# Seventeen unread TensorE products around the first attention scores of layer 1, in a four-layer float32 network on one core

## The chip, the core and the metric

The kernel runs on one core of a Trainium2 chip. The metric is the device time of one execution in microseconds (us); lower is better. Three runs of the kernel before took 2797.55, 2802.72 and 2804.87 us, so the median is 2802.72 us. Besides, one execution was taken by the hardware profiler; all positions below ("at 519 us") are microseconds from the start of that execution's span.

## What is computed

Four layers work on `x` of shape (8, 512, 128), in float32. Each layer is half a feed-forward step, an attention step and half a feed-forward step again, each on a layer-normalised copy:

```python
x = x + 0.5 * L0_ffn(norm(x));  x = x + L0_attn(norm(x));  x = x + 0.5 * L0_ffn(norm(x))
x = x + 0.5 * L1_ffn(norm(x));  x = x + L1_attn(norm(x));  x = x + 0.5 * L1_ffn(norm(x))
...                                                          # layers 2 and 3 likewise
```

The stretch that matters here is the passage from the end of layer 0 to layer 1's attention. That attention has 16 heads of width 8 with rotary positions:

```python
q, k, v = heads(x @ Wq + bq), heads(x @ Wk + bk), heads(x @ Wv + bv)
q, k = rope(q), rope(k)
probs = softmax(q @ k.T / sqrt(8))
out = probs @ v  ->  merged heads @ Wo + bo
```

L1's feed-forward step routes each token to one of 64 small splines by two rounds of scores, a table lookup and an argmax, and normalises its result.

## The kernel before

The input is held on chip as eight blocks `x[b]`, each of 512 rows as 128 partitions x 4 x 128. A normalised copy of block b is `xn[b]`, and its transpose is `xt[b]` (128 partitions, 512 columns). TensorE's order of work is written out by hand in two ways: a dictionary `todo` maps a place (a number) to the steps that are issued there, and it is run in ascending order of places.

*The passage*, `l0_tail` (L810), fetches layer 0's second expert results, adds them, normalises the blocks by pairs (`pair`, L203) and runs the front of L1's feed-forward step for all blocks. For blocks 0 and 1 it also runs the whole step (`l1_ffn_steps`, L920): for block 1 its later places are 55.5 (`turn`, L986, two transposes on TensorE and a copy on ScalarE), 57.5 (`spline`, whose table is a product at L996), 60 (`direct`, a second table product and VectorE work), 62.5 (the statistics, `measure` at L161 on VectorE and GpSimd, then ScalarE, L842) and 69 (`update`, VectorE, L1030 and L1031). Block 0 enters the attention from the list `enter`: at 51.5 its normalised copy is transposed (L237), at 52.5 and 53.5 it is projected to q and k (`project`, L1086: two products each at L1092, rotation on VectorE at L1098 and L1101, then a write to DRAM and a read back into `q` or `k` through SyncE's DMA queue), and at 55 to v (`values`, L1109). The PSUM tiles of the passage come from one pool of seven banks, handed out in turn.

*The attention*, `l1_block` (L1038), goes through 128 units, four for each of the four head groups of each of the eight blocks. In a unit `first` (L1124) is called twice (h = 0 and 1). Each call makes one score tile of two heads, 128 queries by 512 keys each, in one of two PSUM buffers, and VectorE reduces it to the row maxima (L1131). The products of `first` contract over 32 partitions, of which nine are in use. A product in float32 shows as two MATMUL records in the trace, so a unit has eight records of L1130. Eleven units later (`LAG`) `second` (L1145) makes the transposed scores again, with the maxima already subtracted, and ScalarE takes their exponential. So the first eleven units consist of `first` alone, with a few steps of the feed-forward of block 2 and the entry of block 1 between them (`works`). The dictionary of these steps is also called `todo`, and its key is 2n + h for unit n. At key 1 it has `outset` (L1115), which makes a bias with one product (L1120) and one VectorE addition (L1121).

[...]

Of the kernel before, what the change touches and what calls it, by code (L numbers as in the profile page):

```python
# [108 lines left out]
class Net:  # L109
# [700 lines left out]
    def l0_tail(self, w1, wk, bank, room, clear, enter):  # L810

        todo = {}
        load, both, add = self.returned(wk, self.yds[1], 4)

        def at(n, work, *args):
            todo.setdefault(n, []).append(lambda: work(*args))

        for g in range(4):
            n = 9 * g
            for k in range(2):  # L820
                b = 2 * g + k
                at(n - 30, load, b)
                at(n + 1.3 * k, both, b)
                at(n + 1.5 + 1.3 * k, add, b)
                squeeze, finish = self.l1_ffn_front(b, w1, bank, lambda name, shape, k=k: wk.tile([P, *shape], F32, tag=f"{name}{k}", name=name))
                self.plan(todo, (n + 16 + 1.5 * k, n + 19 + 1.5 * k), lambda _, b=b, squeeze=squeeze: squeeze(self.xt[b]), finish)
            self.pair(todo, g, n + 3.5, bank)
        at(20, clear, 0)
        at(46, clear, 1)
        for b, n in ((0, 0), (1, 26)):  # L830
            twin = lambda name, shape: wk.tile([P, *shape], F32, tag=name, name=name)
            self.plan(todo, [n + k for k in (14.7, 17, 18, 19.5, 20.5, 21.7, 23.5, 24.5, 25.5, 27, 28, 29.5, 31.5, 34, 36.5, 43)],
                      *self.l1_ffn_steps(b, w1, bank, twin if b else room, self.xn[b], self.xt[b], self.soon))
        self.plan(todo, (44.5, 51.5, 52.5, 53.5, 55), lambda _: self.soon(0, self.xn[0]), lambda xn: self.turned(xn, bank, self.xt[0]), *enter)
        self.run(todo)

    def soon(self, b, out, src=None):

        src = self.x[b] if src is None else src
        nb, rs = self.measure([src], True)  # L840
        for i in range(4):
            self.nc.scalar.activation(out[:, i, :], src[:, i, :], AF.Identity, bias=nb[:, i : i + 1], scale=rs[:, i : i + 1])  # L842
        return out
# [194 lines left out]
    def l1_block(self, w, w2, room, pool_w):  # L1038
# [18 lines left out]
        with ExitStack() as c:  # L1057
# [10 lines left out]
                nc.sync.dma_start(out=s[8], in_=a["zero"].rearrange("(h n) -> h n", n=512))  # L1068
                scrs.append(s)
            nms, prs, ats = {}, {}, {}  # L1070
            later, todo, bo = {}, {1: [lambda: outset()]}, []

            def clear(n):
                nc.gpsimd.memset(qs[n], 0.0)
# [5 lines left out]
            def bank(name, shape=(P, 512)):  # L1080
                return ps.tile(list(shape), F32, tag="s2", name=name, bufs=4)
# [33 lines left out]
            def outset():  # L1115

                made = pool.tile([P, 2, P], F32, tag="bo", name="bo")
                nc.gpsimd.tensor_scalar(made[:, 0, :], self.const("ones"), self.col("l1_bv"), None, ALU.mult)
                bp = bank("bp", (P, P))
                nc.tensor.matmul(bp, lhsT=made[:, 0, :], rhs=wv[:, 1, :], start=True, stop=True)  # L1120
                nc.vector.tensor_tensor(made[:, 1, :], bp, self.row("l1_bo"), ALU.add)  # L1121
                bo.append(made[:, 1, :])
# [79 lines left out]
            for b in range(NB):  # L1202
                n = 32 * b
# [6 lines left out]
            for b in range(2):  # L1210
                n = 32 * (NB + b) - 50
# [3 lines left out]
            n = 32 * NB - 50 + 32  # L1215
# [664 lines left out]
```

## Time and profile before

| what | value |
|---|---|
| median of three runs | 2802.72 us |
| the profiled execution's own time | 2823.91 us |
| its span, first to last instruction | 2821.98 us |
| mean granted TensorE clock | 0.939 |
| busy: TensorE, VectorE, ScalarE, GpSimd | 89%, 67%, 62%, 42% |
| passage (`l0_tail`) | about 417 to 519 us |
| first scores alone (units 0 to 10) | 519 to 569 us |
| TensorE and VectorE busy from 519 to 569 us | 44.6 and 32.0 of 50 us |
| granted clock from 519 to 569 us | 0.50 |

How to read it: the profiled execution takes some 21 us more than the median run, so a sum of durations is made against 2823.91 us, and only its difference is carried over. "Granted clock" is the share of TensorE's full clock that it was allowed in a stretch; in this trace it takes the values 0.50 and 1.00, and a number between them is a mean over both. PE is TensorE, PEld its loading of weights, DVE VectorE, ACT ScalarE, POOL GpSimd and SPq the queue of SyncE, which issues DMAs. In a row of the timeline, `x8` is the number of records merged into it, and a bracket at its end gives how long the engine sat idle before and who ended that.

### The profile page before, as it was taken

How to read it: one execution, taken by the hardware profiler on the slowest of the kernel's cores; microseconds unless marked ns; L12 is line 12 of the kernel's file. 1: busy time of each engine (PE TensorE's matmuls, PEld its weight loads, DVE VectorE, ACT ScalarE, POOL GpSimd, SP SyncE). 2: the span in 40 equal slices, each digit the busy share in tenths (PEclk: the TensorE clock that was granted, in tenths of full speed). 3: DMA queues.
4: the chain of work that ended last, by engine and by line, in shares of the span. 5: the costliest groups of instructions: out<-in, count | busy, mean ns of one | idle time of the engine just before them, and what ended most of it. 6: DMA issues, size and time to landing. Idle time of an engine off the chain costs nothing.

```text
span 2822.0 us, 51514 instructions
## 1 busy us (share of the span) xinstructions
PE 2508.1 (89%) x18564; PEld 1500.6 (53%) x18564; DVE 1886.6 (67%) x5099; ACT 1741.5 (62%) x4302; POOL 1177.3 (42%) x2073
## 2 busy tenths in 40 slices
PE   5667685799999998899999999999989999999996
PEld 5445453333333343456566656566555666666663
DVE  5235424677777763465666666655589888998897
ACT  2124124166666665676666666666578888988884
POOL 5644356333333442225425344250244454554442
PEclk9877785599999998999999999999999999999998
DMA  8121132000000000000000000000000000000000
GB/s 255 42 68 32 41 89 74 17 17 18 21 19 19 10 18 4 31 1 1 1 1 1 1 1 1 1 1 1 16 9 9 17 20 17 9 17 20 20 2 12
DMA packets 74349, 67.28 MB, mean 24 GB/s; under 512 B 17760, under 2 KB 63848, under 8 KB 71880
## 3 DMA queue, kind: packets, MB, share of 16 engines
q1 hardware_dynamic: 66128, 51.44, 6.8%
q0 software_dynamic: 3872, 8.11, 1.1%
q10 hardware_dynamic: 4096, 4.44, 0.5%
q8 instruction: 148, 2.42, 0.4%
q14 instruction: 105, 0.86, 0.1%
HBM read 36.68 MB, written 27.33 MB: 23 GB/s over the span
## 4 chain that ended last, share of the span: by engine, by line
PE 52%; DVE 16%; ACT 10%; POOL 4%; issue 2%; DMA 0%; SPq 0%; POOLq 0%; ACTq 0%; DVEq 0%
PE tp L1313 7%; PE s L1287 5%; PE s L1130 5%; PE o L1602 4%; PE o L1160 4%; ACT e L1560 4%; PE o L1329 4%; DVE nm L1131 4%; PE s L1553 3%; DVE nm L1291 3%; PE yp L308 3%; PE tp L1579 2%; DVE x L310 2%; PE op L1616 2%; ACT pt L1581 2%
## 5 line engine op out<-in xcount | busy, mean ns | idle before, releaser
L1131 DVE TENSOR_REDUCE nm<-s 128x2 f32<-128x1024 f32 x256 | 305.7, 1218 | 126.7 <-PE s L1150 114.1
L1298 ACT ACTIVATE e<-s,nm 128x512 f32<-128x512 f32 x512 | 344.9, 688 | 26.8 <-DVE nm L1291 22.2
L1152 ACT ACTIVATE pr<-s 128x512 f32<-128x512 f32 x512 | 272.2, 599 | 116.6 <-PE s L1150 106.4
L1319 ACT ACTIVATE p<-tp 128x512 f32<-128x512 f32 x512 | 279.3, 616 | 69.2 <-PE tp L1313 69.2
L1130 PE MATMUL s<-k,q 32*128 32x512 f32 x1024 | 291.4, 676 | 33.6 <-DVE nm L1131 29.2
L1291 DVE TENSOR_REDUCE nm<-s 128x2 f32<-128x1024 f32 x256 | 301.0, 1217 | 27.7 <-PE s L1287 25.8
L1313 PE MATMUL tp<-cst,e 128*128 128x128 f32 x2048 | 293.6, 282 | 24.7 <-DVE rs L1304 14.3
L1313 PEld LDWEIGHTS tp<-cst,e 128*128 128x128 f32 x2048 | 220.4, 142 | 163.0 <-issue 97.8
L1150 PE MATMUL s<-q,k 32*128 32x512 f32 x1024 | 292.1, 639 | 10.4 <-ACT pr L1152 8.6
L1307 POOL TENSOR_SCALAR e<-e,rs 128x512 f32<-128x512 f32 x114 | 199.8, 1753 | 235.5 <-DVE rs L1304 196.0
L1560 ACT ACTIVATE e<-e,m 128x512 f32<-128x512 f32 (+3 forms) x512 | 286.1, 570 | 14.1 <-DVE m L1557 14.0
L1557 DVE CUSTOM_DVE_ANT_0 e<-s,bias 128x512 f32<-128x512 f32 (+3 forms) x512 | 220.1, 486 | 76.6 <-PE s L1553 76.3
L173 POOL TENSOR_TENSOR d<-st 128x4 f32<-128x4 f32 (+2 forms) x97 | 19.8, 204 | 557.1 <-DVE st L170 478.1
L1581 ACT COPY pt<-tp 128x512 f32<-128x512 f32 x320 | 173.8, 590 | 83.4 <-PE tp L1579 83.3
L1307 DVE TENSOR_SCALAR e<-e,rs 128x512 f32<-128x512 f32 x398 | 195.4, 521 | 9.1
L310 DVE SCALAR_TENSOR_TENSOR x<-yp,sel,x 128x128 f32<-128x128 f32 x512 | 178.0, 348 | 31.4 <-PE yp L308 18.8
L1287 PE MATMUL s<-k,q 32*128 32x512 f32 x1024 | 175.1, 648 | 4.8 <-issue 2.5
L1553 PE MATMUL s<-qk 64*128 64x512 f32 (+3 forms) x1024 | 172.7, 456 | 3.1 <-DVE m L1557 2.0
L1579 PE MATMUL tp<-cst,e 128*128 128x128 f32 x1280 | 169.1, 278 | 4.3 <-ACT k L1021 2.6
L1130 PEld LDWEIGHTS s<-k,q 32*128 32x128 f32 x1024 | 88.5, 195 | 153.0 <-DVE nm L1131 102.8
L1329 PE MATMUL o<-p,va 128*32 128x128 f32 x4096 | 165.4, 277 | 2.6 <-ACT p L1319 2.6
L1579 PEld LDWEIGHTS tp<-cst,e 128*128 128x128 f32 x1280 | 139.8, 142 | 39.0 <-issue 14.8
(408 smaller groups left out, 4981.9 us busy)
## 6 DMA issues: line engine op xcount, KB each, us to landing
yd<-z SPq DMA_DIRECT2D x8, 1024.0 KB
r<-yd SPq DMA_DIRECT2D x32, 256.0 KB
xd<-xn SPq DMA_DIRECT2D x16, 256.0 KB
k<-sk SPq DMA_DIRECT2D x64, 64.0 KB
sk<-pu SPq DMA_DIRECT2D x16, 256.0 KB
w<-in_l_w SPq DMA_DIRECT2D x14, 256.0 KB
q<-sq SPq DMA_DIRECT2D x32, 72.0 KB
x<-in_x SPq DMA_DIRECT2D x8, 256.0 KB
```

The source lines that it names most:

```text
L1130: nc.tensor.matmul(s[:, jj, :], lhsT=q[cut, g, i * P : (i + 1) * P], rhs=k[cut, g, :], start=True, stop=True)
L1131: nc.vector.tensor_reduce(nms[b, g // 2][:, i, 2 * h : 2 * h + 2, g % 2], s, AX.X, ALU.max, negate=True)
L1150: nc.tensor.matmul(s, lhsT=k[cut, g, kt * P : (kt + 1) * P], rhs=q[cut, g, :], start=True, stop=True)
L1287: nc.tensor.matmul(s[:, jj, :], lhsT=q[cut, g, i * P : (i + 1) * P], rhs=k[cut, g, :], start=True, stop=True)
L1291: nc.vector.tensor_reduce(nm, scores[n, h], AX.X, ALU.max, negate=True)
L1298: nc.scalar.activation(e, s[:, jj, :], AF.Exp, bias=nm[:, jj : jj + 1], accum_out=sm[:, jj : jj + 1])
L1307: (nc.gpsimd if h and jj and n >= 14 else nc.vector).tensor_scalar(e, e, rc[:, jj : jj + 1], None, ALU.mult)
L1313: nc.tensor.transpose(tp[:, kt, :], probs[n][j][:, kt * P : (kt + 1) * P], self.ident)
L1319: nc.scalar.activation(p, turns[n].pop(0), AF.Exp)
L1329: nc.tensor.matmul(o[32 * j : 32 * j + 32, g * P : (g + 1) * P], lhsT=vas[b % 2][:, kt, 4 * g + j, :], rhs=p2[j][:, kt, :], start=(kt == 0 ...
L1560: outs.append(lambda e=e, jj=jj: nc.scalar.activation(e, e, AF.Exp, bias=mins[n][:, jj, i : i + 1], scale=-1.0, accum_out=sums[n][:, jj, i ...
L1579: nc.tensor.transpose(tp[:, k, :], block(n, jj, i, kt), self.ident)
```

## The change

A method `idle` takes one PSUM bank and multiplies the identity by `xt[1]`, 128 x 128 by 128 x 512, n times into that bank. Nobody reads the bank. The method is called at four places of the passage with n = 1, 3, 1 and 6, and at key 1 of the attention, behind `outset`, with n = 6. Each product shows as two MATMUL records of 128 rows and 512 columns. Nothing is removed and nothing is moved.

```diff
@@ l0_tail
+
+        for n, k in ((51.6, 1), (55.2, 3), (55.6, 1), (62, 6)):
+            at(n, self.idle, bank, k)
         self.plan(todo, (44.5, 51.5, 52.5, 53.5, 55), lambda _: self.soon(0, self.xn[0]), lambda xn: self.turned(xn, bank, self.xt[0]), *enter)
         self.run(todo)
+
+    def idle(self, bank, n):
+        t = bank("hot")
+        for _ in range(n):
+            self.nc.tensor.matmul(t, lhsT=self.ident, rhs=self.xt[1], start=True, stop=True)
@@ l1_block
-            later, todo, bo = {}, {1: [lambda: outset()]}, []
+            later, todo, bo = {}, {1: [lambda: outset(), lambda: self.idle(bank, 6)]}, []
```

So on TensorE's queue one product stands between the transposes of block 0 (L237) and its projection (L1092), three between the values (L1112) and block 1's `turn` (L989), one between that and the first table (L996), six between the second table and the first scores (L1130), and six between unit 0, with the bias product L1120, and unit 1.

## The prediction

> **What bounds the kernel here.** First the page's slices, to see where the array is slow; then the chain of waits, to see what sets the pace there; then busy time in short stretches that run from one change of the granted clock to the next (the changes in this trace all lie on one grid of 3.41 us).
>
> ```profile
> PE   5667685799999998899999999999989999999996
> PEclk9877785599999998999999999999999999999998
> ```
>
> Slices 7 and 8 (423 to 564 us) stand at little over half the clock, the second of them with TensorE 0.7 busy. That is where layer 1's attention starts: 519 to 569 us, the scores of L1130 alone, until the second scores (L1150) join at 569.05. The chain of waits there is a two-step loop:
>
> ```profile
> 523.54 0.70 DVE z L1030
> 524.33 0.70 DVE x L1031
> 525.12 1.24 DVE nm L1131
> 526.40 2.10 PE s L1130 x4
> 528.52 1.24 DVE nm L1131
> 529.80 2.10 PE s L1130 x4
> 531.93 1.24 DVE nm L1131
> ```
>
> One score tile (2.10), its maximum (1.24), and the next tile in the same buffer: one unit each 3.405 us (528.52 to 531.93). It is a loop of latencies; neither engine is full. In the timeline at full clock the loop is shorter:
>
> ```profile
> 581.27 3.67 DVE L1131 TENSOR_REDUCE nm<-s 128x2 f32<-128x1024 f32 x3
> 582.55 0.70 PE L1130 MATMUL s<-k,q 32*128 32x512 f32 x2 [0.95 <-DVE nm L1131]
> 583.08 0.59 PE L1130 MATMUL s<-k,q 32*128 32x512 f32 x2
> ```
>
> The tile takes 583.67 - 582.55 = 1.12 us, and the first and third maximum, which use one buffer, start 3.67 - 1.22 = 2.45 us apart. So the full clock would save 3.405 - 2.45 = **0.955 us a unit**, over ten units (1 to 10). That is all the change can win. The question is how long the clock stays up.
>
> ```profile
> core 0: us, PE busy (x) PEld busy (x) DVE busy (x) ACT busy (x) POOL busy (x), PEclk, DMA share, GB/s
> 504.52:507.93 3.41, 3.41 (x5) 1.35 (x4) 2.66 (x5) 0.00 (x0) 0.00 (x0) 0.50 0.00 0
> 507.93:511.34 3.41, 1.63 (x10) 1.05 (x8) 3.20 (x10) 0.58 (x1) 0.00 (x0) 1.00 0.44 127
> 511.34:514.76 3.42, 2.02 (x10) 1.32 (x10) 1.54 (x8) 0.37 (x1) 0.00 (x0) 1.00 0.57 112
> 514.76:518.17 3.41, 0.00 (x0) 0.00 (x0) 2.47 (x11) 0.00 (x0) 0.59 (x4) 1.00 0.32 58
> 518.17:521.58 3.41, 2.69 (x6) 1.58 (x7) 0.00 (x0) 0.00 (x0) 2.73 (x10) 0.50 0.17 22
> ...
> 528.41:531.82 3.41, 3.22 (x12) 1.01 (x8) 2.36 (x2) 0.00 (x0) 0.67 (x1) 0.50 0.01 2
> 531.82:535.24 3.42, 3.23 (x12) 1.00 (x8) 2.36 (x2) 0.00 (x0) 0.00 (x0) 0.50 0.00 0
> ...
> 955.08:958.49 3.41, 1.81 (x15) 0.75 (x16) 3.38 (x8) 0.59 (x2) 2.59 (x10) 1.00 0.00 0
> 958.49:961.90 3.41, 3.41 (x10) 0.46 (x4) 2.04 (x2) 2.59 (x5) 3.05 (x8) 0.50 0.00 0
> ```
>
> Read the clock of a row as the verdict on the row before it. One stretch full of projections (L1092) raises it; an empty one (514.76) lowers it just as the scores begin. The scores fill 94% of their stretches and never raise it. I count what is streamed: columns of each MATMUL record, times rows in use over 128. An L1092 record has 512 columns and took 6.59/8 = 0.82 us cold, so a full cold stretch streams about 2,100. A score record uses 32 of 128 rows, so a unit (8 records) counts 8 x 512/4 = 1,024, one cold stretch 1,026. Counted over the trace's stretches, full-row work kept the clock from about 1,500 up (511.34 has 1,800) and lost it below about 1,470. Score work lost it at 955.08 with about 1,600 (1,467 from the records; one of a group of four is missing), and kept it at 579.61 with 1,720. At full clock, scores alone would stream 1,024 x 3.41/2.45 = **1,430 a stretch: too little**.
>
> **The change part by part.** Seventeen products of the identity with xt[1], five banks taken, no copy, no DMA, no semaphore anybody waits for. One product is like half of the warm pair of L1092 (two products in 1.98 us), so about 0.9 us in a row, or 2 x 0.82 = 1.65 us cold.
>
> A, one product after the turn of block 0 (L237, ends 499.6). The projection waits 2.49 us there for the copy xt. 1.65 us fit; cost nothing. It may bring the clock up one stretch earlier, so that the projection (6.59 cold) runs warm; the vector engine's rotations (L1098) follow it with other work between, and only the 0.69 us it waits at 505.89 could go. I take 0 and keep -0.7.
>
> B, three products after the values (L1112, end 509.55), at full clock since 507.93: 2.7 us against a wait of 2.36 us for sel: the turn L989 is late by about 0.3. C, one product between L989 and the table L996: 0.9 us against a gap of 0.46: 0.4 more. These 0.7 us go down the chain hh, mg, z, statistics, POOL, z (L842), L1030, L1031 to the first maximum: 525.12 becomes 525.8, and the buffer for unit 1, which came at 526.40, comes at 527.1.
>
> D, six products after the second table (end 514.4, now 515.1): 5.4 us, to 520.5. The gap before the scores is 4.5 us and ends with k's landing (518.89), so unit 0 starts 1.6 us late, but its maxima cannot start before 525.8: hidden, with 4 us to spare. D fills the empty stretch, so the clock holds.
>
> E, six products behind unit 0 and L1120: unit 0 warm takes about 1.3 us (520.5 to 521.8), L1120 0.4, then E to 527.6. Unit 1 could start at 527.1: so 0.5 late by E, 1.2 in all against 526.40. Its tile takes 1.12 in place of 2.10 us, so its first maximum is at about 528.8 against 528.52: **+0.3**. If the cover of the late L1031 were gone, E would cost its whole 5.4.
>
> Then the gain. The stretch in which E ends passes (0.1 us of dense products is enough beside the scores); the next one holds scores alone, 1,430, and the clock drops at its end. The grid's phase against the kernel isn't fixed, so warm time after E is 3.4 to 6.8 us, 5.1 in the middle. Less the first tile, (5.1 - 1.1)/2.45 = 1.6 loops at 0.955 = **-1.6 us** (0.9 to 2.2). After that the units run at 3.405 again, as before.
>
> Sum: +0.3 - 1.6 = -1.3, with part of A's -0.7 about **-1.5 us**. Against the profiled execution's own 2823.91 us that is 2822.4; I carry the difference over to the median of the runs, 21 us lower: 2802.7 - 1.5 = 2801.2. From 569 us on the engines follow each other without any clock time in between, so the shift should reach the end.
>
> **A rule against the trace.** The Trainium skill, TensorE: Matmul & The Clock Gate, section "Why this matters for your kernels", says to keep TensorE continuously busy for 4 us or more to get the fast clock and to leave no idle gap over about 3 us to keep it. By that, once E has raised the clock the scores, whose waits are under 1.2 us, would hold it to the end: the first rival. But by the same rule the 50 us from 519 to 569, with no wait over 2.2 us, should have risen by themselves, and they stand at 0.50. Rows in use must count; I take the rows of the trace.
>
> **The rivals.**
> *The clock holds.* Units 1 to 6 save 6 x 0.955 = 5.7, the signature product L933 (1.88) half. From 547 to 569 the chain has 16 us of TensorE, half of which could go, but the vector engine has 16 us of its own there in 22, so at most 5.5. Together 5.7 + 0.9 + 5.5 - 0.3 = 12 us: 2791. For it: 1,430 is only some 5% under what full-row work kept. Against: scores at 1,600 lost it.
> *Slower: the products run cold.* Each of D's and E's twelve then takes 0.8 us more, some 10 us; less the 0.5 us of slack left and with B and C late by 1 to 3 us: about 2814. It decides as soon as the clock is at half when D starts (a phase in which the projection's stretches fall short). Against: the 6.6 us of L1092 and then B always fill one whole stretch of the grid.
> *Nothing moves.* Gains and delay cancel, or the scores lose the clock at E's end: within a microsecond of 2802.7. For it: gain and cost are both under 2 us.
>
> **How the numbers follow.** Short warm time 0.62 (2801.2, own range 2797 to 2806, as the runs spread by 7 us), holds 0.17, nothing 0.09, cold 0.12. The range reaches the holding case's 2791 and, on the other side, the runs' spread and a part of the cold case: 2791 to 2808. This kernel's measurement tells about 0.3% (8.4 us) from no change. Faster by that: nearly all of "holds" and a little more, 0.17; slower: the cold case and a little, 0.13; within, 0.70.
>
> **What would show it.** Clock 1.00 from about 505 us to some 5 us behind E, then 0.50 until the projection of block 1; maxima 2.45 us apart for one to two units, then 3.4; first maximum at 525.8, unit 1's at 528.8; scores of unit 0 at 520.5. Wrong if the clock stays 1.00 until 569 (holds), if a product of D or E takes 1.65 us (cold), or if the stage from 500 to 569 us is shorter or longer by over 4 us.

## The result, and the profile after

The kernel with the products took 2799.2 us (median of 20 runs, 2793.54 to 2805.3), the kernel before 2804.05 us on the same chip (20 runs, 2797.55 to 2808.8). The ratio on record is 0.9986, with a 95% interval of 0.998 to 0.9992: 3.9 us faster, with an interval of 2.2 to 5.6, inside the 0.3% that was called no change. (The two medians alone differ by 4.85 us, also inside that interval.) The forecast was 1.5 us faster.

The profiled execution of the changed kernel took 2798.31 us, its span is 2796.3 us and the mean granted clock 0.945. Its passage starts 28 us earlier than in the profile before, a difference that arises in layer 0, where the instructions of the two kernels are the same. So positions are not compared, only stretches of the same work. All line numbers in the attention are eight higher: the scores are L1138, the maxima L1139, the bias product L1128, the added products L843.

First the page's slices of the changed kernel: busy tenths of TensorE and tenths of the granted clock, 70 us a slice.

```profile
PE   5857667899999997999999999999999999999996
PEclk9978776799999998999999999999999999999998
```

Slice 8 (489 to 559 us) is the one to look at: it starts just ahead of the first scores. It can't be set against slice 8 of the page before, which starts 25 us ahead of them. The stretch of the profile before that begins at the same work and is as long goes from 517.29 to 587.19 us; here it is (columns: us, busy us and records of PE, PEld, DVE, ACT and POOL, granted clock, DMA share, GB/s), first before, then changed:

```profile
517.29:587.19 69.90, 61.03 (x226) 22.59 (x230) 46.74 (x66) 16.26 (x31) 20.29 (x39) 0.63 0.09 18
489.40:559.30 69.90, 62.49 (x254) 22.25 (x256) 46.80 (x65) 16.37 (x32) 19.87 (x37) 0.78 0.08 18
```

TensorE is about as busy, 62.5 us in place of 61.0, with 28 records more, most of them added products, and its clock has gone from 0.63 to 0.78. VectorE gets through 65 instructions in place of 66: a higher clock by itself is not yet a gain. Next the chain of waits of the changed kernel in order of time (start us, us, what).

```profile
480.78 2.58 PE hot L843 x6
483.36 0.35 PE tp L997 x2
483.71 0.86 PE hot L843 x2
484.57 1.31 PE pa L1004 x8
485.88 5.15 PE hot L843 x12
...
491.14 2.94 PE s L1138 x8
494.08 0.42 PE bp L1128 x2
494.50 5.15 PE hot L843 x12
499.65 1.08 PE s L1138 x8
...
500.76 1.24 DVE nm L1139
...
502.04 1.15 PE s L1138 x4
...
503.21 1.24 DVE nm L1139
```

Before, this chain went through VectorE to the first maximum (L1030, L1031) and from there around the loop. Now it goes down TensorE's own queue: three products, the turn, one product, the table, six products, unit 0, the bias and six products again, with 0.10 us between that no work fills (491.03 to 491.14, in a row left out here). Two things are read from it. A tile is computed in 1.15 us instead of 2.10, so the clock is up. And unit 0 took 2.94 us, though it too ran at full clock. It has four products, one for each head, and each needs one of the four parts in which k is read back. The last three parts landed at 491.03, 492.05 and 492.85 us, and the four products start at 491.14, 491.26, 492.09 and 492.99. So the six products behind it (E) begin late and end at 499.65.

Who waits for that is seen in VectorE's line of the timeline (start, us, engine, line; the two maxima of unit 0 are merged into one row).

```profile
496.61 2.36 DVE L1139 TENSOR_REDUCE nm<-s 128x2 f32<-128x1024 f32 x2
```

One maximum takes 1.22 us, and in the profile before TensorE started 0.06 us after the end of the one it waited for (526.40 against 525.12 + 1.22). So the buffer for unit 1 was free at 496.61 + 1.22 + 0.06 = 497.89. TensorE came for it at 499.65, 1.7 us later. From unit 0's first maximum to unit 1's it is 4.15 us (496.61 to 500.76) against 3.40 before.

Last the clock: the stretches of the changed kernel along the grid of 3.41 us.

```profile
core 0: us, PE busy (x) PEld busy (x) DVE busy (x) ACT busy (x) POOL busy (x), PEclk, DMA share, GB/s
496.27:499.69 3.42, 3.42 (x12) 1.25 (x11) 2.80 (x4) 0.00 (x0) 0.38 (x1) 1.00 0.00 0
499.69:503.10 3.41, 2.10 (x12) 0.50 (x12) 2.34 (x2) 0.00 (x0) 0.89 (x1) 1.00 0.02 7
503.10:506.51 3.41, 3.21 (x14) 0.90 (x12) 3.21 (x4) 0.00 (x0) 0.00 (x0) 1.00 0.00 0
506.51:509.93 3.42, 3.33 (x10) 1.01 (x8) 2.46 (x3) 0.00 (x0) 0.00 (x0) 0.50 0.00 0
```

The clock rose at 479.21, stayed at 1.00 through the passage, unit 0 and E, and fell at 506.51, 6.9 us behind E. The stretch before the fall, 503.10, has TensorE 94% busy. It holds scores alone, and counted as in the prediction (columns times rows in use over 128) they stream 1,438 columns, against the 1,430 worked out. The stretch before that counts 1,439, all but the same, and it kept the clock; the last record of E ends only 0.04 us ahead of its edge. Why the one kept the clock and the other lost it is not shown. In this profile the exception gave a second warm loop.

### The profile page after: what moved, and what is told of

Read it like the earlier page. It is cut to its first block, busy times and chain, and to the rows that moved or that the text cites. A ratio compares the mean times of both kernels' runs of the same rounds, so it can differ in the third digit from the quotient of the medians.

```text
span 2796.3 us, 51582 instructions
## 1 busy us (share of the span) xinstructions
PE 2505.9 (90%) x18598; PEld 1496.0 (53%) x18598; DVE 1887.8 (68%) x5099; ACT 1741.0 (62%) x4302; POOL 1178.6 (42%) x2073
## 4 chain that ended last, share of the span: by engine, by line
PE 54%; DVE 16%; ACT 10%; POOL 4%; issue 2%; DMA 1%; SPq 0%; POOLq 0%; ACTq 0%; DVEq 0%
PE tp L1321 8%; PE s L1295 6%; PE s L1138 5%; PE o L1610 4%; PE o L1168 4%; ACT e L1568 4%; PE o L1337 4%; DVE nm L1139 4%; PE s L1561 3%; PE yp L308 3%; DVE nm L1299 3%; PE tp L1587 2%; PE op L1624 2%; ACT pt L1589 2%; DVE x L310 2%
## 5 line engine op out<-in xcount | busy, mean ns | idle before, releaser
L1139 DVE TENSOR_REDUCE nm<-s 128x2 f32<-128x1024 f32 x256 | 305.9, 1218 | 125.9 <-PE s L1158 114.7
L1138 PE MATMUL s<-k,q 32*128 32x512 f32 x1024 | 285.2, 659 | 29.4 <-DVE nm L1139 29.0
L1138 PEld LDWEIGHTS s<-k,q 32*128 32x128 f32 x1024 | 85.8, 191 | 146.7 <-DVE nm L1139 101.2
```

Of the source, the lines that this page charges most:

```text
L1138: nc.tensor.matmul(s[:, jj, :], lhsT=q[cut, g, i * P : (i + 1) * P], rhs=k[cut, g, :], start=True, stop=True)
L1139: nc.vector.tensor_reduce(nms[b, g // 2][:, i, 2 * h : 2 * h + 2, g % 2], s, AX.X, ALU.max, negate=True)
```

## The experiments

Each kernel differs from the changed one by the lines shown. The levels of the sets (the medians of the kernel before) differ by up to 38 us, so every ratio is to the kernel before within its own set. Beside the time I read two stretches from each profile. VectorE's instructions are the same in all these kernels, so **the stage** runs from its first statistics of the passage to the instruction that stands at 608 us in the profile before, and **the tail** from there to the end.

| kernel | ratio to before (95%) | stage us | tail us | first maxima, unit 0 to 1, us |
|---|---|---|---|---|
| before, two profiles | | 175.34, 174.39 | 2213.9, 2216.9 | 3.40 |
| the change | 0.9986 (0.998 to 0.9992) | 173.96 | 2217.5 | 4.15 |
| the change, second | 0.9998 (0.9987 to 1.0008) | 174.30 | 2217.2 | 3.90 |
| the change, third | 0.9989 (0.998 to 0.9999) | 174.83 | 2223.8 | 3.94 |
| passage only (A to D) | 0.9991 (0.998 to 1.0003) | 175.76 | 2221.7 | 3.40 |
| unit 0 only (E) | 1.0001 (0.999 to 1.0012) | 176.59 | 2216.9 | 5.89 |
| products over 32 rows | 1.0037 (1.0027 to 1.0047) | 190.20 | 2220.5 | 13.23 |
| kept warm | 0.9979 (0.9969 to 0.9989) | 171.32 | 2219.3 | 4.21 |
| kept warm, again | 0.9985 (0.9973 to 0.9998) | 171.03 | 2219.2 | 3.88 |
| held | 0.9992 (0.9978 to 1.0006) | 168.39 | 2223.1 | 3.37 |
| held, with late fillers | 1.0 (0.9988 to 1.0012) | 174.68 | 2226.0 | 3.99 |
| twelve behind unit 0 | 1.0023 (1.0014 to 1.0031) | 180.18 | 2221.4 | 9.17 |
| four behind unit 0 | 0.9992 (0.9982 to 1.0003) | 171.16 | 2216.5 | 2.47 |

The tails spread over 12 us, though the work in them is the same except in the one kernel with late fillers. So one profile can show what happens in the stage, but not what a kernel gains to within a few microseconds.

**Half of the change: passage only.** E is taken away.

```diff
-            later, todo, bo = {}, {1: [lambda: outset(), lambda: self.idle(bank, 6)]}, []
+            later, todo, bo = {}, {1: [lambda: outset()]}, []
```

> The eleven products of the passage alone, none behind unit 0. Short-warm theory: the clock is up when the scores begin, the stretch of unit 0 and its wait for the late maxima is too thin (1,024 full-row columns at most), and the clock falls within one or two stretches, before the maxima of units 1 and 2 gain much: 0 to 1.5 us faster than before, so 2 to 4 us slower than the changed kernel if the products behind unit 0 carry the gain of about 4 us. Rival, the gain sits in the passage (its projection and tables run at the full clock): as fast as the changed kernel, ratio to before 0.9986.

Timeline of this kernel, the scores of units 1 and 2 after the maxima of unit 0:

```profile
530.11 3.21 PE L1138 MATMUL s<-k,q 32*128 32x512 f32 x8 [4.84 <-DVE nm L1139]
```

Unit 1 waits for the first maximum, as in the kernel before (there 2.11 us, here 4.84, since unit 0 is done sooner), and its tiles are cold (at half clock): the stretch with unit 0 and this wait streamed 922 counted columns, and the clock was gone before unit 1. Without E nothing is won in the loop, so the stage is no shorter than before (175.76 us against 175.34 and 174.39). But the time ratio, 0.9991, can't be told from the whole change's. So the times alone don't show that E earns anything.

**The other half: unit 0 only.** The four places of the passage are taken away.

```diff
-        for n, k in ((51.6, 1), (55.2, 3), (55.6, 1), (62, 6)):
-            at(n, self.idle, bank, k)
```

> The six products behind unit 0 alone. Short-warm theory: they start at half clock (the passage leaves it at 0.50 when the scores begin), so they take up to 10 us in place of 5.3 and push unit 1 back by 2 to 7 us; the warm loops after them win back 1 to 2: 0 to 5 us slower than before. Rival, the clock follows at once and the passage's products are not needed: 1 to 2 us faster than before.

Timeline of this kernel (the added products are L841 here, the scores L1136):

```profile
524.66 6.38 PE L841 MATMUL hot<-xt,cst 128*128 128x512 f32 x12
530.97 1.14 PE L1136 MATMUL s<-k,q 32*128 32x512 f32 x8
```

E starts cold, takes 6.38 us instead of 5.32 and raises the clock itself, at 526.80. Unit 1 is then warm, but it starts at 530.97, while the first maximum began at 526.26: the gap between the maxima is 5.89 us. The two warm loops of 2.45 us that follow don't pay for that; the stage is 1.25 us longer than in the first profile before. So in these profiles D's job is to keep E short, and E's is to lend its clock to the next units; neither half has a gain in the stage by itself.

**Do the rows in use count, or busy time?** The same products in the same places, over 32 rows instead of 128.

```diff
-            self.nc.tensor.matmul(t, lhsT=self.ident, rhs=self.xt[1], start=True, stop=True)
+            self.nc.tensor.matmul(t, lhsT=self.ident[0:32, :], rhs=self.xt[1][0:32, :], start=True, stop=True)
```

> The same seventeen products over 32 rows in place of 128: the same number of records and columns, the same time on TensorE. Rows count: they stream a quarter, 512 to 1,024 full-row columns a stretch, so the clock falls to 0.50 before or within them, each product takes up to 1.7 us and unit 1 starts up to 8 us later: 4 to 10 us slower than before. Rival, busy time counts whatever the rows: clock and time as with the change, 0.9986 of before.

Two stretches of this kernel in the place of D (columns as in the windows above), and E in its timeline:

```profile
515.48:518.89 3.41, 3.41 (x6) 1.20 (x6) 2.69 (x12) 0.00 (x0) 0.43 (x3) 0.50 0.43 77
518.89:522.31 3.42, 3.42 (x6) 1.34 (x5) 0.00 (x0) 0.00 (x0) 2.69 (x11) 0.50 0.02 2
```

```profile
529.92 9.75 PE L843 MATMUL hot<-xt,cst 32*128 32x512 f32 x11
```

TensorE is busy without a gap for both stretches, 6.8 us, and the clock stays at 0.50. Four such records stream as many columns as four wide ones, but counted by rows they are 512 in the second stretch, and 746 in the first, which has the end of the second table in it. E ran cold at 9.75 us and more (one of its twelve records stands apart), and the kernel lost 0.37%. This is what the rival "the products run cold" describes; it was forecast at 2814 - 2802.7 = 11 us, and 0.37% of 2834 is 10.5 us. (In the one profile the stage is 15 us longer.) Busy time alone does not raise the clock; the rows in use must count.

**Lending the clock for longer: kept warm.** A half product of 256 columns behind each of units 1 to 8.

```diff
-    def idle(self, bank, n):
+    def idle(self, bank, n, cols=512):
...
-            self.nc.tensor.matmul(t, lhsT=self.ident, rhs=self.xt[1], start=True, stop=True)
+            self.nc.tensor.matmul(t[:, 0:cols], lhsT=self.ident, rhs=self.xt[1][:, 0:cols], start=True, stop=True)
...
+            for m in range(1, 9):
+                todo.setdefault(2 * m + 1, []).append(lambda: self.idle(bank, 1, 256))
```

> The change, and one further product of 256 columns and 128 rows behind each of units 1 to 8 (512 full-row columns each). If about 1,500 full-row columns a stretch hold the clock, 1,430 of the scores plus 512 x 3.41/2.45 = 713 hold it at 1.00 through to the second scores; unit starts 2.45 us apart or little more (the products cost 0.43 us each in waits of TensorE); the stage before the second scores shortens by 7 to 10 us against before, ratio to before about 0.9970. Rival, the loop of score and maximum is delayed by each product and the clock was not the limit: no faster than the change, 0.9986 or above.

```profile
538.60:542.01 3.41, 3.41 (x16) 1.34 (x16) 2.95 (x4) 0.00 (x0) 0.00 (x0) 1.00 0.00 0
542.01:545.43 3.42, 3.42 (x18) 1.72 (x18) 2.50 (x3) 0.29 (x1) 0.00 (x0) 1.00 0.00 0
545.43:548.84 3.41, 3.41 (x11) 1.48 (x10) 1.88 (x2) 0.00 (x0) 0.00 (x0) 0.50 0.00 0
```

In these stretches of the kernel the clock holds to unit 5 and is lost at 545.43. In the stretch before that stand eight records of a step of block 2's feed-forward, of eight columns each, and the count is 1,349, though TensorE was busy all the time. Four maxima in a row on VectorE, two units, are one row of its timeline:

```profile
535.31 4.81 DVE L1139 TENSOR_REDUCE nm<-s 128x2 f32<-128x1024 f32 x4 [0.46 <-PE s L1138]
```

Two units take 4.81 + 0.46 = 5.27 us, 2.64 each, so a half product costs some 0.2 us a unit, and the loop still gains 0.77. The stage is 4.0 us shorter than in the first profile before, and 4.3 in the second run of the same kernel, below. I had expected a clock held through unit 8.

**Is the change's own size sure?** The changed kernel once more, without an edit, and later a third time.

> The changed kernel a second time, for another phase of the clock's grid and another set of runs. Short-warm theory: clock up from the projection to 3.4 to 6.9 us after the last product of unit 0, then half again; the stage from the first statistics of the passage to well behind the second scores 1 to 3 us shorter than in the profile of before; ratio 0.9986 within its interval. Rival, the -1.4 us of the first profile is the whole gain: a ratio of 0.9995.

> The changed kernel a third time, for the size of its gain: between the first measurement (0.9986) and the second (0.9998). My sum says 1.5 us, 0.9995; the stage up to 608 us 0.4 to 2 us shorter than in the two profiles of before.

The three ratios are 0.9986, 0.9998 and 0.9989, mean 0.9991, or 2.5 us of gain; the interval of the second has 1 in it. The clock fell 6.9, 3.7 and 4.3 us behind E, and there were two, one and one warm loops of 2.45 us.

**Holding it to the end of the stage: held.** The products are set so that every stretch should count more than 1,500.

```diff
-        for n, k in ((51.6, 1), (55.2, 3), (55.6, 1), (62, 6)):
+        for n, k in ((51.6, 1), (55.2, 2), (62, 6)):
...
-            later, todo, bo = {}, {1: [lambda: outset(), lambda: self.idle(bank, 6)]}, []
+            later, todo, bo = {}, {1: [lambda: outset(), lambda: self.idle(bank, 5)]}, []
...
+            for m, k in ((1, 1), (2, 1), (3, 1), (4, 1), (5, 2), (6, 3), (7, 4), (8, 3)):
+                todo.setdefault(2 * m + 1, []).append(lambda k=k: self.idle(bank, k, 256))
```

`idle` has the argument `cols` as above.

> Passage 1, 2 and 6 products (the one between turn and table left out), 5 behind unit 0, and behind units 1 to 8 products of 256 columns: 1, 1, 1, 1, 2, 3, 4, 3. In the run that kept the clock up to unit 5 it fell in the stretch with the eight small signature products, which streamed only 1,350 full-row columns. Rows count: with these every stretch up to unit 8 has over 1,700, the clock holds to about unit 9, and the stage is 6 to 9 us shorter than before: ratio about 0.9970. Rival, the further products sit in the loop of units 5 to 8 and eat what the clock gives: no better than the run before, 0.9979 or above.

In the stage it did what was expected: 6.95 us shorter than the first profile before, 6.0 than the second. The ratio of the times is 0.9992, and its interval, 0.9978 to 1.0006, holds the whole 6 us as well as nothing. Beside it, in the same set, ran the kernel before for one more profile.

> The kernel before, for a second profile of it. Both theories: clock down from the first or second score stretch to the projection of block 1; the stage from the first statistics of the passage to the second scores within 2 us of the first profile (how much the phase alone moves it).

The two profiles end within 0.1 us of each other (spans of 2791.0 and 2791.1 us), so they show where the gain went in this execution. Up to 905 us the held kernel keeps its lead of 6.3 us; by 1,019 us, where the same instruction starts within 0.01 us in both, it is gone. One stretch of 116 us of each, first of the held kernel, then of the kernel before, in which the same work comes 6 us later:

```profile
900.00:1016.00 116.00, 107.16 (x678) 44.69 (x678) 72.65 (x129) 67.46 (x130) 57.50 (x117) 0.90 0.05 11
```

```profile
906.00:1022.00 116.00, 107.58 (x711) 45.52 (x712) 78.23 (x141) 71.86 (x138) 58.80 (x118) 0.94 0.05 11
```

The kernel before stands at 0.94 and gets through 711 records of TensorE and 141 instructions of VectorE; the held one stands at 0.90 and gets through 678 and 129. It is 33 records and 12 instructions behind in equal time. By the times at which the clock changes it spends 23.9 us there at half clock, against 13.7: 10 us more. As records take twice as long at half clock, that can cost 5 us by my estimate, so not quite the whole lead. None of the added products lies there. That the earlier start moved this work against the grid, and that this brought the dips, is likely but not shown.

Nor does the pair show what happens on the average. Every run has its span and clock on record, which gives its time at half clock: in the mean 286 us for the held kernel and 329 us for the kernel before in the same set. That is 43 us less, not much short of the 47 us by which the two profiles differ in the stage alone. So, as far as two profiles can tell, on the average little was given back by the clock.

The profile of the kernel before has one more use: nothing was changed, and its stage is 0.95 us shorter than in the first one. Of this, 0.77 us arises at the second rotation of the first projection (L1098, at 505.89 us in the first profile), which is where I had kept 0.7 us as a possible gain of A.

**Can the lost clock be brought back?** The held kernel with full products at three places near the dip (`for at, k in ((201, 3), (237, 1), (239, 1))`, added to `todo` in the same way).

> The run that held the clock through unit 8, with five more products of 512 columns near the end of the attention: three at place 201 and one each at 237 and 239, where the profiles show thin stretches (clock down for 3 to 14 us between 951 and 1047). If the gain of that run (7.0 us up to 930 us) was given back there by lower clock, this keeps it: 5 to 7 us of it are left at 1,060 us, ratio 0.9975. Rival, the giving back is not of the clock, or the products cost as much: no better than that run's 0.9992.

The ratio is 1.0 and the tail 2226.0 us, the longest of all. In this execution the stage itself was only 0.66 us shorter than in the first profile before: the same products, at another phase, lost the clock in the passage and at units 8 to 10. The fillers didn't bring the expected gain: the interval, 0.9988 to 1.0012, leaves 0.9975 out. Nor did they change the time at half clock: over the runs of the set it is 43 us below that of the kernel before, as it was without them. What sets the dips there stays open: the extra time at half clock was seen in one profile, and no edit removed it.

**The price of E: more and fewer products behind unit 0.** Twelve, then four, in place of six, by the number in the `idle` call at key 1:

```diff
-            later, todo, bo = {}, {1: [lambda: outset(), lambda: self.idle(bank, 6)]}, []
+            later, todo, bo = {}, {1: [lambda: outset(), lambda: self.idle(bank, 12)]}, []
```

> Twelve products behind unit 0 in place of six. My sum: six fill a wait that is there anyway, six more find no cover and cost 5.1 us in full (0.85 each), and the warm time behind them is the same: 5 us slower than the change, ratio to before about 1.0004. Rival, the warm time or its start grows with the number of products: less than 3 us slower.

> The change with four products behind unit 0 in place of six. In the profile of the change the chain runs through these products: they end 1.7 us after VectorE has freed the buffer for unit 1. Two products fewer are 1.7 us: the first maximum of unit 1 then comes 2.4 to 2.6 us after that of unit 0's first, against 4.15 with six and 3.40 before, the clock is held as before since the stretch still streams over 1,500 columns, and the stage is 1 to 1.7 us shorter than with the change. In the time that is 0.0005 of a ratio and hardly seen. Rival, another wait (VectorE's bias addition, the bank) takes the place: 3.4 us or more between the two maxima.

Timelines, first with twelve, then with four (the fill, and with four the maxima of unit 0 and the next ones):

```profile
491.91 10.46 PE L843 MATMUL hot<-xt,cst 128*128 128x512 f32 x24
```

```profile
493.40 3.60 PE L843 MATMUL hot<-xt,cst 128*128 128x512 f32 x8
495.72 2.36 DVE L1139 TENSOR_REDUCE nm<-s 128x2 f32<-128x1024 f32 x2
498.19 4.80 DVE L1139 TENSOR_REDUCE nm<-s 128x2 f32<-128x1024 f32 x4
```

The fill of twelve takes 10.46 us in place of 5.32, 5.1 us more, and the first gap is 9.17 us, 5.0 to 5.3 more than in the three profiles with six. So every further product lands whole on the gap. The ratio is 1.0023, about 7 us over the change in the same set (0.9998) and 9 over the mean of its three; what makes it more than 5.1 is not shown. With four, the fill ends at 497.00, just as the buffer comes free (495.72 + 1.22 + 0.06), and the first gap is 498.19 - 495.72 = 2.47 us, that of a warm loop. So two of E's six products had no cover. The stage of this run is 2.8 us shorter than the change's first one, more than those two products (1.7 us): where block 1 is projected the clock came back sooner in this execution, and there the lead grows by some 1.6 us. The time, 0.9992, can't be told from the change's.

**Kept warm, again.** The same kernel as before, in another set.

> The run with one product of 256 columns behind each of units 1 to 8 a second time. If its 0.9979 was the kernel's and not the day's: 0.9979 within its interval, 3 to 5 us shorter than before up to 608 us in the profile. Rival, the later stages take it back in most executions: 0.999 or above.

Its ratio of 0.9985 and the 0.9979 before are the best measured, 4 to 6 us below the kernel before. The intervals reach to 0.9998 and 0.9989, and those of the change's first and third run lie over them, so I can't call it better than the change.

## Why the prediction was right, step by step

**Right:** the time (2801.2 forecast, 2799.2 measured), roughly the gain (1.5 us against 2.5 in the mean of three measurements, 3.9 in the first), and the order of events: the clock up before the scores, held through D and E, one or two loops at 2.45 us, then 3.41 again.

**A** cost nothing, and it gained nothing that was shown. The 0.7 us kept as a possible gain turned up in a profile of the kernel before, without any added product; so it is not shown to be A's.

**B and C** were to make the first maximum 0.7 us late. B cost 0: it ended as sel came. C cost 0.23 us (1.14 us between turn and table against 0.91 in the profiles before). Counted from sel, the first maximum was late by about 0.15 us.

**D** was hidden, as forecast, and filled the empty stretch. With the products cut to 32 rows the clock stayed down there.

**E is the term that was mis-sized.** The sum said "unit 0 warm takes about 1.3 us", that E would make unit 1 "0.5 late", and that unit 1's first maximum would be +0.3. A tile at full clock takes about 1.1 us, but what unit 0's two tiles need was not there at once: with k's four landings unit 0 took 2.94 us, E ended 1.7 us after the buffer came free, and the first gap grew from 3.40 us to between 3.90 and 4.15. By the sum it should have shrunk to 528.8 - 525.8 = 3.0 us, so E was taken about 1 us too small. B and C were taken half a microsecond too large, and the two errors cancel in part. With the first maximum late by 0.15 that makes unit 1 0.75 late on the mean of three profiles ((0.74 + 0.50 + 0.54) / 3 + 0.15), not 0.3. I had read the start of the first score (518.89), which follows the first landing, as the end of the wait for k; the last of the four landings sets it. The profile before has it in its timeline, where unit 0 takes 4.67 us though two cold tiles alone take 2 x 2.10 = 4.2:

```profile
518.89 4.67 PE L1130 MATMUL s<-k,q 32*128 32x512 f32 x8 [4.50 <-POOL ve L178]
```

Four products behind unit 0 show the term gone: 2.47 us.

**The gain** was forecast at 1.6 loops x 0.955 us. Two, one and one loops, 1.3 in the mean, is 1.3 us; so the sum by the profiles is +0.75 - 1.3, about half a microsecond faster, and at the fifth unit the three profiles are indeed half a microsecond ahead of the first profile before, counted from sel. At 608 us 0.2 us of it are left. The means of the stages, 174.36 us for the change and 174.87 for the kernel before, also differ by half a microsecond, but 0.4 of this is the wait at the second rotation, which only one of the two profiles before has; against the other, 174.39, nothing is left. The measured mean is 2.5 us faster. What lies between, some 2 us, no profile here shows, because the tail of a single execution differs by up to 12 us from another's; **it stays open**. The passage alone has the same ratio, 0.9991, without any warm loop, so the times don't show that the gain comes from the loops. That the forecast came near the measured gain is therefore in part luck.

The prediction also said that ten units at 0.955 us are all the change can win, 9.6 us. Its own rival came to 12, and only the first six gaps between units in the profile before are the plain loop of 3.40 us; the next four have other steps in them and take 4.95, 5.19, 4.25 and 3.5.

**The rivals.** *The clock holds*, which follows from the rule of busy time in the Trainium skill (TensorE: Matmul & The Clock Gate, section "Why this matters for your kernels": no idle gap over about 3 us), fell: in the stretch at 503.10 us TensorE was 94% busy, no wait behind E was over 1.31 us, and the clock went at the end of that stretch. Here the measurement decides. The 32-row run fell the same way, without any gap. *The products run cold* didn't happen in the profiles of the change, and its price was measured with the 32-row products at 10.5 us, near the forecast. *Nothing moves* fits one of the three measurements (0.9998), and the forecast's own range of 2797 to 2806 would not tell it apart.

## What to carry to other kernels

In these profiles, filling idle TensorE time lent its clock to work that came within one or two clock stretches, so count what the following stretch streams, by rows in use, before paying for it. Size a fill by the last of the waits that it hides behind: with several tiles landing one after another, the last landing decides, and products beyond the cover cost their whole length. And where the gain is a few microseconds, measure the same kernel more than once and take two profiles of the kernel before: the phase alone moved this stage by 1 us, and the tail of the unedited changed kernel by 6.6.

## What was not expected of the hardware

The granted clock followed a count, not busy time. I counted full-row columns in every stretch of all fourteen profiles, each record shared out by its time among the stretches that it touches, and took the 5,473 stretches whose products all have outputs of full width (128 columns). A stretch at half clock was followed by full clock in none of 683 cases below 1,500 columns, in 12 of 24 between 1,500 and 1,600, and in all 247 from 1,600 up. A stretch at full clock was followed by full clock in 4 of 356, 21 of 30 and all 4,133. So up and down have the same mark, near 1,540, within the error of the count, and one stretch decides: all changes lie on the grid of 3.41 us.

The count has a limit. Where products have outputs of 32 columns, as those of L1168, it fails: in the profile of the change the stretch at 1011.69 us counts 5,210 and the clock was still at half behind it. What such products count for is not shown here.

The grid runs free of the kernel: from the start of the span to its first edge it is 0.06 us in one profile and 3.33 in another. In one pair of executions a lead of 6.3 us from layer 1 was gone some 450 us later, with 10 us more at half clock, in work that had not been changed. So a kernel whose stages stream close to this mark can have a time that depends on where its stretches fall, and a local gain need not last to the end.
